# The last two token tiles of the q, k, v projection made key first, and the late key rows ahead of the values' copy

## The chip, the cores and the metric

The kernel runs on one core of a Trainium2 chip. The metric is the device time of one execution in microseconds (us), and the kernel's time is the median of several. Five engines work side by side, each with a queue of its own that it goes through in order: TensorE (PE in the profile, its weight loads PEld), VectorE (DVE), ScalarE (ACT), GpSimd (POOL) and SyncE (SP). SP, POOL and, rarely, ACT also issue the DMAs. A tile in PSUM is written by TensorE and has to be read out ("evicted") before its bank is used again.

## What is computed

A transformer block with modulation by a condition, for x of 2 x 2048 x 576 in float32, 16 heads of 36:

```python
xn = _ln(x, 1e-06)
xn = xn * (1 + sc_msa[:, None, :]) + sh_msa[:, None, :]
qkv = (xn @ w_qkv + b_qkv).reshape(B, N, 3, H, hd)
q, k, v = (qkv[:, :, 0], qkv[:, :, 1], qkv[:, :, 2])
q = _ln(q, 1e-05, qn_g, qn_b)
k = _ln(k, 1e-05, kn_g, kn_b)
attn = jnp.einsum('bqhd,bkhd->bhqk', q, k) * scale
attn = jax.nn.softmax(attn, axis=-1)
o = jnp.einsum('bhqk,bkhd->bqhd', attn, v).reshape(B, N, C)
o = o @ w_proj + b_proj
x = x + g_msa[:, None, :] * o
...
h = jax.nn.gelu(xn2 @ w1 + b1, approximate=False)
m = h @ w2 + b2
x = x + g_mlp[:, None, :] * m
```

The change lies where the making of q, k and v ends and attention begins, once in each of the two batches, and in one place near the end of batch 0's attention.

## The kernel before

**Projection** (`inputs`, lines from L1045). A batch has 2048 tokens in 16 tiles of 128 (NT = 16). For each tile TensorE makes three products, q, k and v (`product`, L1101 and L1103), each in two halves of 288 columns, into a PSUM tile `s` of two banks; there are four such tiles in turn. The weights have been centred, so that the mean of each head is already zero and the normalization needs only the variance:

- `biased` (L1115 for q and k, L1118 for v): VectorE evicts a product, adding the bias. q and k go to `both`, v goes straight to its place for attention, `vt`.
- `squared` (L1055): ScalarE squares q and k into `sq`, of which there is one buffer.
- `head_scale` (L1060 to L1067): VectorE sums the squares of each head (`var`), ScalarE takes the root, VectorE the reciprocal (`inv`), and POOL multiplies q and k by it.
- `by_feature` (L1080, L1082): VectorE transposes blocks of 32 x 32 into `turned_qk` (three buffers), and four DMAs write the rows by feature to a DRAM tensor, `qk`. They are issued by SP, or by POOL where the call says so.

Of tile t, `head_scale` runs one tile later and `by_feature` two tiles later. Key rows are read back from DRAM block by block (`take_k_block`: tiles 0-3, 4-7, 8-11, 12-13, 14-15) by SP's DMAs (L812, L814), to `km0` (32 of the 36 features of each head) and `ke0` (the other four). The DMAs are issued behind the writes of the block's last tile (for tiles 12-13 behind those of tile 14), and `take_k_block` returns a function, `made`, that applies gain and bias (L847) and splits `ke` in a high and a low part (L847, L856, L857): four VectorE operations. A list, `taken`, keeps such functions. A later `by_feature` with `ready=True` runs what is in it; with `ready=False` it doesn't. For the last tile the order is k, q, v, and its key rows are written apart from its q rows, by POOL's queue. The functions for tiles 12-13 and 14-15 are left over and returned to attention.

**Attention** (`attend`, L1228 to L1291) goes through 8 pairs of heads (p), 4 blocks of 512 queries (qb) and 4 groups of keys (g): 128 steps. Step (p, qb, g) computes the scores of two blocks of 128 keys from each half of the sequence: tiles 2g, 2g + 1, 8 + 2g and 9 + 2g. So the first two steps want tiles 8 to 11, the third 12 and 13, the fourth 14 and 15. Scores go to banks of PSUM taken from a ring of eight (`bank`), four per block of keys; ScalarE takes the exponentials to `pt` (L1232, five buffers of two); the products with `vt` (L1241) come one step behind the scores, into the next bank of the ring, and VectorE adds them to `ot` (L1291, or a copy, L1289, for the first group). VectorE's other work in attention is kept in a list, `later`, that says at the end of which step it is put in the queue; `hooks` holds further work by step. The two left functions came in through the hook of step (0, 0, 0) and went to the front of `later` for the next two turns: each behind the copy or add of the step. The closing 1/sum of a query block is `divided` (L1260, L1261).

**Order.** In both stages the order on VectorE and POOL is that of the source (a manual schedule), in the projection also on SP, in attention also on ScalarE. The rest is ordered by the scheduler. Buffers and banks are handed out as the scheduler sees them come free. Near the end of batch 0's attention three tiles of the next batch's input get their statistics (L1327, L1328) at steps (7, 2, 0), (7, 2, 1) and (7, 2, 2); `rows_turned` uses them after the last step.

Of the kernel before, what the change touches and what calls it, by code (L numbers as in the profile page):

```python
# [8 lines left out]
F32 = mybir.dt.float32  # L9
# [7 lines left out]
P = 128  # L17
# [14 lines left out]
def dit_block(  # L32
# [25 lines left out]
    nc = tc.nc  # L58
    B, N, C = x.shape
# [3 lines left out]
    NT = N // P  # L63
# [688 lines left out]
    def block_of_small():  # L752
# [292 lines left out]
        def inputs(b, weights, making, work, xnts, turned, loaded):  # L1045

            wq, wq4, bq = weights
            both, squares, taken = {}, {}, []
            key_blocks = {3: (0, 4), 7: (4, 8), 11: (8, 12), NT - 2: (12, 14), NT - 1: (14, NT)}

            def squared(t, w0=0, w1=2):
                if squares.get("t") != t:
                    squares.update(t=t, sq=work.tile([P, 2 * C], F32, name="sq", bufs=1))
                part = slice(w0 * C, w1 * C)
                nc.scalar.activation(squares["sq"][:, part], both[t][:, part], AF.Square)  # L1055

# [108 lines left out]
                    q = two_steps(0, t) if t == 0 else product(0, t)  # L1165
                    biased(0, q, t)

            for t in range(NT - 1):
                modulated_ahead(t)
                begun(t)  # L1170
                if t >= done:
                    q = product(0, t)
                k = product(1, t) if t >= done else two_steps(1, t)
                if t >= done:
                    biased(0, q, t)
                if b == 0 and t == 0:
                    xnts[done] = input_loaded(turned.pop(done), nc.gpsimd)
                    turned_ahead(t + 1)
                turned_ahead(t)
                biased(1, k, t)  # L1180
                if t > 0:
                    head_scale(t - 1)
                if t >= done:
                    v = product(2, t)
                    biased(2, v, t)
                if b == 0 and t == TPB + 1:
                    kept()
                if t >= 2:
                    by_feature(t - 2)
                squared(t)  # L1190

            t = NT - 1
            k, q, v = (product(w, t) for w in (1, 0, 2))
            head_scale(t - 1)
            by_feature(t - 2)
            biased(1, k, t)
            squared(t, 1, 2)
            head_scale(t, 1, 2)
            by_feature(t - 1, ready=False)
            biased(0, q, t)  # L1200
            squared(t, 0, 1)
            by_feature(t, 1, 2, ready=False, queue=nc.gpsimd)
            head_scale(t, 0, 1)
            biased(2, v, t)
            by_feature(t, 0, 1, ready=False)
            return taken

        NG = NT // 4

        def attend(b, pool, hooks):  # L1210

            def scores(p, qb, g):
                i, j = p % 2, qb % 2
                pts = []
                for k0 in (2 * g * P, (2 * g + 1) * P):
                    keys = slice(k0, k0 + P)  # L1220
                    banks = [bank() for _ in range(4)]
                    for k, q, first in (
                        (km[i], qm[j], True),
                        (ke[i].bitcast(F32R), qe[j].bitcast(F32R), False),
                    ):
                        for r0, ps in zip(range(0, P, 32), banks):
                            r = slice(r0, r0 + (DIMS if first else 4 * (HD - DIMS)))
                            nc.tensor.matmul(ps, k[r, keys], q[r, :], start=first, stop=not first)  # L1228
                    for c in range(2):
                        pt = pool.tile([P, 2, BLK], F32, name="pt", bufs=5)  # L1230
                        for h in range(2):
                            nc.scalar.activation(pt[:, h, :], banks[2 * c + h], AF.Exp, scale=SCALE)  # L1232
                        pts.append((pt, k0 // P + c * NT // 2))
                return pts

            def values(p, pts):
                acc = bank()
                for pt, kc in pts:
                    for h in range(2):
                        v0 = (kc * H + 2 * p + h) * HV  # L1240
                        nc.tensor.matmul(  # L1241
                            acc[64 * h : 64 * h + 64, :],
                            vt[:, v0 : v0 + 64],
                            pt[:, h, :],
                            start=pt is pts[0][0],
                            stop=pt is pts[-1][0],
                        )
                return acc

            def finish(p, qb, ot):  # L1250


                den = pool.tile([P, BLK], F32, name="den")
                for h in range(2):
                    sums = den_dram[b, p, qb, h, :]
                    nc.sync.dma_start(out=sums.unsqueeze(0), in_=ot[64 * h + HD : 64 * h + HD + 1, :])
                    nc.sync.dma_start(out=den[64 * h : 64 * h + 64, :], in_=sums.partition_broadcast(64))

                def divided():
                    nc.vector.reciprocal(den, den)  # L1260
                    nc.vector.tensor_tensor(ot, ot, den, ALU.mult)  # L1261
                    cols = slice(qb * BLK, (qb + 1) * BLK)
                    for h in range(2):
                        for c, row, d, n in head_rows((2 * p + h) * HD):
                            for r in (row,) if c < FULL else (row, row + 64):
                                nc.sync.dma_start(
                                    out=held["qo"][r : r + n, c, cols], in_=ot[64 * h + d : 64 * h + d + n, :]
                                )

                return divided  # L1270

            steps = [(p, qb, g) for p in range(NPAIR) for qb in range(NBLK) for g in range(NG)]


            behind, later = None, [[] for _ in range(13)]
            for p, qb, g in [*steps, (None, None, None)]:
                pts = None if p is None else scores(p, qb, g)
                if g == 0 and (p, qb) != (NPAIR - 1, NBLK - 1):
                    for i, do in enumerate(take_q(*((p, qb + 1) if qb + 1 < NBLK else (p + 1, 0)))):
                        later[1 + i].append(do)  # L1280
                if g == 1 and qb == 0 and p + 1 < NPAIR:
                    for i, do in enumerate(take_k(p + 1)):
                        later[3 + NG * i].append(do)
                if behind is not None:
                    bp, bqb, bg, bpts = behind
                    acc = values(bp, bpts)
                    if bg == 0:
                        ot = pool.tile([P, BLK], F32, name="ot", bufs=2)
                        nc.vector.tensor_copy(ot, acc)  # L1289
                    else:  # L1290
                        nc.vector.tensor_tensor(ot, acc, ot, ALU.add)  # L1291
                    if bg == NG - 1:
                        later[2 if bp == NPAIR - 1 else 3].append(finish(bp, bqb, ot))
                if (p, qb, g) in hooks:
                    due = hooks[p, qb, g]() or []
                    later[1] = due[:1] + later[1]
                    later[2] = due[1:] + later[2]
                later.append([])
                for do in later.pop(0):
                    do()  # L1300
                behind = (p, qb, g, pts)
            for do in [do for group in later for do in group]:
                do()
# [127 lines left out]
        for b in range(B):  # L1431
# [32 lines left out]
            def output_opened():  # L1464
                opening["wp"] = output_weights(b)

            hooks = {
                (0, 0, 0): lambda: left,
                (4, 0, 1): output_opened,
            }  # L1470
            hooks |= {
# [2 lines left out]
            if b + 1 < B:  # L1474
                begun = [(spare[5 + t], x[b + 1, t * P : (t + 1) * P, :], spare[8 + t]) for t in range(3)]

                def rows_opened():
                    opening["begun"] = rows_begun(begun)
                    for i in range(len(begun)):
                        opening["begun"][0](i)  # L1480

                def rows_turned():
                    opening["turned"] = opening["begun"][2]()

                hooks |= {(7, 1, 1): rows_opened, (None, None, None): rows_turned}
                hooks |= {
                    (7, 2 + i // NG, i % NG): lambda i=i: opening["begun"][1](i) for i in range(len(begun))
                }
            if b == 0:
                hooks |= {  # L1490
# [5 lines left out]
            with tc.manual_schedule(  # L1496
                engines={mybir.EngineType.DVE, mybir.EngineType.Pool, mybir.EngineType.Activation}
            ):
                attend(b, att, hooks)
            close_att()  # L1500
            close_psum()
            close_psum = opened_psum(s=4)
# [400 lines left out]
```

## Time and profile before

| | us |
|---|---|
| runs of the kernel | 3148.82 median of 3 (3148.65 to 3154.48) |
| the profiled execution | 3152.0 |
| its span in the profile | 3150.2 |
| TensorE's granted clock over the span | 0.999 |
| projection of batch 0, to the first score | 0 to 240.4 |
| first five steps of attention, batch 0 | 240.4 to 269.6 |
| first score of batch 1 | 1303.47 |
| DMA, mean over the span | 99 GB/s |

The costliest groups of instructions, with the sum and the mean of one, are the exponentials (L1232: 1057.6, 610 ns), the value products (L1241: 935.0, 598 ns), the scores (L1228: 571.9 and 422.1) and the projection's products (L1101: 404.9). A line of a timeline has the start, the time taken, the engine, the line of the source and the operation, output<-input, the shape, and the number of instructions merged; in brackets stands how long the engine had been idle before it, and who ended that. Matmuls are pipelined, so groups overlap a little. In a line of the busy table the three figures are busy time, share of the span and number of instructions.

### The profile page before, as it was taken

The page shows a single profiled execution, that of the slowest core. Times are in us where ns is not written, and L with a number is a line of the kernel's source. Part 1 is how long each engine was busy: PE and PEld are TensorE (multiplying, and loading weights), DVE is VectorE, ACT ScalarE, POOL GpSimd, SP SyncE. Part 2 cuts the span into 40 slices and gives each one's busy share as a digit, 9 for nine tenths or more (in the row PEclk, how much of TensorE's full clock was granted, in tenths as well). Part 3 has the DMA queues.
Part 4 walks back from the last instruction along what each step waited for, and adds up shares of the span by engine and source line. Part 5 has one row for each costly group of instructions (what it writes and reads, how often), then busy time and mean ns, then how long its engine had stood idle before and what let it go on. Part 6 is the DMA issues. An engine that isn't in the chain of part 4 may idle for free. (4 is left out here: it accounts for less than half of the span.)

```text
span 3150.2 us, 46743 instructions
## 1 busy us (share of the span) xinstructions
PE 3125.2 (99%) x17553; PEld 1862.0 (59%) x17553; DVE 1515.6 (48%) x2181; ACT 1471.2 (47%) x2843; POOL 664.2 (21%) x932
## 2 busy tenths in 40 slices
PE   8999999999999999999999999999999999999999
PEld 5883333333333788633333333368888888777777
DVE  6653443444344556434443444445566554545454
ACT  2326666666666122466666666633555541000000
POOL 4641000011110455200011111013333320112111
PEclk9999999999999999999999999999999999999999
DMA  5753221132221756411122222146554434333331
GB/s 142 179 96 95 78 64 46 54 80 73 65 74 41 244 101 123 88 45 34 44 62 68 81 65 66 56 159 188 166 132 137 136 109 165 106 121 117 117 105 39
DMA packets 300451, 311.94 MB, mean 99 GB/s; under 512 B 178936, under 2 KB 233080, under 8 KB 298104
## 3 DMA queue, kind: packets, MB, share of 16 engines
q1 hardware_dynamic: 252240, 192.19, 21.2%
q0 software_dynamic: 44432, 111.07, 13.3%
q10 hardware_dynamic: 3544, 5.60, 0.5%
q8 instruction: 141, 2.31, 0.3%
q14 instruction: 94, 0.77, 0.1%
HBM read 191.80 MB, written 106.45 MB: 95 GB/s over the span
## 5 line engine op out<-in xcount | busy, mean ns | idle before, releaser
L1232 ACT ACTIVATE pt<-b 128x512 f32<-128x512 f32 x2048 | 1057.6, 610 | 484.2 <-PE b L1241 271.2
L1241 PE MATMUL b<-pt,vt 128*64 128x512 f32 x4096 | 935.0, 598 | 0.0
L1241 PEld LDWEIGHTS b<-pt,vt 128*64 128x64 f32 x4096 | 271.8, 136 | 582.1 <-issue 438.8
L1228 PE MATMUL b<-qm,km 32*128 32x512 f32 x4096 | 571.9, 614 | 1.0 <-issue 1.0
L1291 DVE TENSOR_TENSOR ot<-b,ot 128x512 f32<-128x512 f32 x192 | 132.8, 692 | 617.5 <-PE b L1241 617.5
L1228 PE MATMUL b<-qe,ke 16*128 16x512 f32 x2048 | 422.1, 788 | 0.0
L1101 PE MATMUL s<-wq,xnt 128*128 128x288 f32 x1536 | 404.9, 407 | 2.1 <-ACT xnt L395 2.1
L1228 PEld LDWEIGHTS b<-qm,km 32*128 32x128 f32 x4096 | 192.3, 184 | 276.8 <-ACT pt L1232 215.6
L1815 PE MATMUL s<-ws,as 128*128 128x288 f32 x1440 | 351.8, 406 | 0.0
L1101 PEld LDWEIGHTS s<-wq,xnt 128*128 128x128 f32 x1536 | 281.5, 190 | 64.7 <-ACT xnt L395 1.6
L1815 PEld LDWEIGHTS s<-ws,as 128*128 128x128 f32 x1440 | 273.6, 190 | 75.6
L1260 DVE RECIPROCAL den<-den 128x512 f32<-128x512 f32 x64 | 213.6, 3337 | 11.1 <-DMA den<-den_dram 11.1
L1655 PE MATMUL m<-xnt,wb 128*128 128x256 f32 x864 | 210.4, 379 | 1.6 <-issue 0.9
L1655 PE MATMUL m<-s,wb 128*128 128x256 f32 x864 | 210.0, 379 | 0.0
L1005 POOL DMA_DIRECT2D turned<-squares x212 | 142.5, 678 | 259.0 <-DVE squares L1000 241.0
L1655 PEld LDWEIGHTS m<-s,wb 128*128 128x128 f32 x864 | 164.2, 190 | 22.3
L1228 PEld LDWEIGHTS b<-qe,ke 16*128 16x128 f32 x2048 | 107.8, 184 | 115.9 <-issue 112.0
L1289 DVE COPY ot<-b 128x512 f32<-128x512 f32 x64 | 44.3, 692 | 272.7 <-PE b L1241 272.7
L1655 PEld LDWEIGHTS m<-xnt,wb 128*128 128x128 f32 x864 | 158.9, 190 | 21.3 <-issue 1.3
L1693 ACT ACTIVATE cs<-cs,b_sb 128x512 f32<-128x512 f32 x144 | 98.9, 719 | 111.8 <-DVE cs L1688 85.8
L812 POOL DMA_DIRECT2D km<-qk x56 | 28.2, 503 | 571.7 <-PE b L1228 568.8
L1022 ACT ACTIVATE xnt<-xnt,mod 128x128 f32<-128x128 f32 x244 | 100.4, 481 | 102.1 <-DMA xnt<-turned 94.6
(206 smaller groups left out, 2941.0 us busy)
## 6 DMA issues: line engine op xcount, KB each, us to landing
gelu<-cs SPq DMA_DIRECT2D x144, 256.0 KB
hidden<-gelu SPq DMA_DIRECT2D x16, 2304.0 KB
x_dram<-spare POOLq DMA_DIRECT2D x64, 288.0 KB, 2.5
qk<-turned_qk SPq DMA_DIRECT2D x120, 144.0 KB
qm<-qk SPq DMA_DIRECT2D x256, 64.0 KB
den<-den_dram SPq DMA_DIRECT2D x128, 128.0 KB
turned<-squares POOLq DMA_DIRECT2D x212, 72.0 KB, 2.5
xnt<-turned POOLq DMA_DIRECT2D x54, 256.0 KB, 4.1
```

What stands on the lines that cost most here:

```text
L1005: queue.dma_start(out=by_square[g], in_=squares[g * SQ : (g + 1) * SQ, :].rearrange("p (k j) -> p k j", j=SQ))
L1022: nc.scalar.activation(part, part, AF.Identity, **affine(which, k, b))
L1101: nc.tensor.matmul(out_a, full[:, k, :], wq[:, k, f], start=k == 0, stop=False)
L1228: nc.tensor.matmul(ps, k[r, keys], q[r, :], start=first, stop=not first)
L1232: nc.scalar.activation(pt[:, h, :], banks[2 * c + h], AF.Exp, scale=SCALE)
L1241: nc.tensor.matmul(acc[64 * h : 64 * h + 64, :], vt[:, v0 : v0 + 64], pt[:, h, :], start=pt is pts[0][0], stop=pt is pts[-1][0],)
L1260: nc.vector.reciprocal(den, den)
L1289: nc.vector.tensor_copy(ot, acc)
L1291: nc.vector.tensor_tensor(ot, acc, ot, ALU.add)
L1655: nc.tensor.matmul(out_m[m], wb[:, slot[m], k, f * P : (f + 1) * P], moving[m](k), start=k == 0 and m in (1, 2, 5, 6), stop=k == 1 and m == 1,
L1693: nc.scalar.activation(part, part, AF.Gelu, bias=b1_sb[:, g : g + 1])
L1815: nc.tensor.matmul(ms[m], stationary[m][:, f, :], ws[m][:, f, :], start=(f == 0), stop=(f == HF - 1))
```

## The change

For tiles 14 and 15 together, the products are made in the order k, k, q, q, v, v. Tiles 13, 14 and 15 are written to DRAM in two parts, keys and q, with the keys first; tile 15's keys still go by POOL's queue. The rows of tiles 8 to 11 are made by VectorE between tile 15's key transpose and tile 14's q statistics. v is evicted last: tile 14's after tile 14's q transpose, tile 15's after tile 15's. `squared` takes a new tile for each part. In attention, the two functions that are left over are put in VectorE's queue right after the scores of steps (0, 0, 0) and (0, 0, 1). In the program that is built, both stand ahead of the copy of step 0's values. The third tile's statistics move from step (7, 2, 2) to (7, 2, 3). SP's queue, which nothing orders by hand in attention, has batch 0's first gate weights (`wa`) and their biases ahead of the loads of the third q block, where one part of `wa` and the biases stood behind them. The compiled order of buffers has tile 14's q transposed into the buffer that tile 15's key rows are written from.

```diff
             def squared(t, w0=0, w1=2):
-                if squares.get("t") != t:
-                    squares.update(t=t, sq=work.tile([P, 2 * C], F32, name="sq", bufs=1))
+                if squares.get("t") != (t, w0):
+                    squares.update(t=(t, w0), sq=work.tile([P, 2 * C], F32, name="sq", bufs=1))
...
-            for t in range(NT - 1):
+            for t in range(NT - 2):
...
-            t = NT - 1
-            k, q, v = (product(w, t) for w in (1, 0, 2))
-            head_scale(t - 1)
-            by_feature(t - 2)
-            biased(1, k, t)
-            squared(t, 1, 2)
-            head_scale(t, 1, 2)
-            by_feature(t - 1, ready=False)
-            biased(0, q, t)
-            squared(t, 0, 1)
-            by_feature(t, 1, 2, ready=False, queue=nc.gpsimd)
-            head_scale(t, 0, 1)
-            biased(2, v, t)
-            by_feature(t, 0, 1, ready=False)
+            t0, t1 = NT - 2, NT - 1
+            modulated_ahead(t0)
+            k0, k1, q0, q1 = (product(w, t) for w in (1, 0) for t in (t0, t1))
+            head_scale(t0 - 1)
+            by_feature(t0 - 2, ready=False)
+            biased(1, k0, t0)
+            squared(t0, 1, 2)
+            by_feature(t0 - 1, 1, 2, ready=False)
+            head_scale(t0, 1, 2)
+            biased(1, k1, t1)
+            squared(t1, 1, 2)
+            by_feature(t0, 1, 2, ready=False)
+            head_scale(t1, 1, 2)
+            biased(0, q0, t0)
+            squared(t0, 0, 1)
+            by_feature(t1, 1, 2, ready=False, queue=nc.gpsimd)
+            v0 = product(2, t0)
+            key_rows = [*taken]
+            for do in key_rows[:-2]:
+                do()
+            head_scale(t0, 0, 1)
+            biased(0, q1, t1)
+            squared(t1, 0, 1)
+            by_feature(t0 - 1, 0, 1, ready=False)
+            v1 = product(2, t1)
+            head_scale(t1, 0, 1)
+            by_feature(t0, 0, 1, ready=False)
+            biased(2, v0, t0)
+            by_feature(t1, 0, 1, ready=False)
+            biased(2, v1, t1)
+            taken = key_rows[-2:]
             return taken
...
-        def attend(b, pool, hooks):
+        def attend(b, pool, hooks, key_rows):
...
                 pts = None if p is None else scores(p, qb, g)
+                if (p, qb) == (0, 0) and g < len(key_rows):
+                    key_rows[g]()
...
             hooks = {
-                (0, 0, 0): lambda: left,
                 (4, 0, 1): output_opened,
             }
...
                 hooks |= {
-                    (7, 2 + i // NG, i % NG): lambda i=i: opening["begun"][1](i) for i in range(len(begun))
+                    (7, 2, (0, 1, 3)[i]): lambda i=i: opening["begun"][1](i) for i in range(len(begun))
                 }
...
-                attend(b, att, hooks)
+                attend(b, att, hooks, left)
```

## The prediction

> **What bounds the kernel now.** I read the busy table first, then the start times of TensorE's groups around each place the change touches, then what ended the waits there. Times are us of the profiled execution, for batch 0; batch 1 repeats them 1063.07 later.
>
> ```profile
> PE 3125.2 (99%) x17553; PEld 1862.0 (59%) x17553; DVE 1515.6 (48%) x2181; ACT 1471.2 (47%) x2843; POOL 664.2 (21%) x932
> ```
>
> TensorE bounds the whole, so only time in which it is held up counts. Its 99% hides such time, since a matmul that has begun counts as busy while the next one's weights wait. So I read the pitch of attention's steps, from one group of value products (L1241) to the next, in TensorE's timeline:
>
> ```profile
> 248.28 3.65 PE L1241 MATMUL b<-pt,vt 128*64 128x512 f32 x16
> ...
> 255.98 3.65 PE L1241 MATMUL b<-pt,vt 128*64 128x512 f32 x16
> ...
> 263.67 3.65 PE L1241 MATMUL b<-pt,vt 128*64 128x512 f32 x16
> ...
> 269.64 3.65 PE L1241 MATMUL b<-pt,vt 128*64 128x512 f32 x16
> ...
> 275.64 3.65 PE L1241 MATMUL b<-pt,vt 128*64 128x512 f32 x16
> ```
>
> Two pitches are 7.70 and 7.69, the next 5.97 and 6.00. The timelines of the weight loads and of VectorE tell why:
>
> ```profile
> 254.45 0.18 PEld L1228 LDWEIGHTS b<-qe,ke 16*128 16x128 f32 x2 [0.81 <-DVE ke L857]
> ```
> ```profile
> 252.01 0.69 DVE L1289 COPY ot<-b 128x512 f32<-128x512 f32 x1 [3.24 <-PE b L1241]
> 252.74 0.42 DVE L847 TENSOR_SCALAR km<-km,gb_at 64x256 f32<-64x256 f32 x1
> ...
> 253.91 0.48 DVE L857 SCALAR_TENSOR_TENSOR ke<-ended,part,high 64x256 fp32r<-64x256 f32 x1
> ```
>
> Step 2's scores need the keys of tiles 12 and 13. VectorE makes them in four operations that stand behind the copy of step 0's values, and that copy waits for TensorE. So TensorE waits for work that is queued behind a wait for TensorE. Step 3 (tiles 14, 15) repeats it.
>
> Before that, ScalarE starts late, as its timeline shows; the exponentials pace the first two steps:
>
> ```profile
> 241.30 0.31 ACT L1063 ACTIVATE var<-var,eps 128x16 f32<-128x16 f32 x1 [0.82 <-DVE var L1060]
> 241.63 1.28 ACT L1232 ACT_TABLE_LOAD   x1
> 242.92 5.01 ACT L1232 ACTIVATE pt<-b 128x512 f32<-128x512 f32 x10
> ```
>
> **The change, part by part.**
>
> *Key rows ahead of the copy.* Nothing is removed; two groups of four VectorE operations go ahead of L1289. Gain: 7.70 + 7.69 - 2 x 5.98 = 3.43 in batch 0; batch 1's pitches, 7.67 and 7.66, give 3.37. **6.80** in all, if the rows are made before step 2's scores (some 250.8 in the new time).
>
> *The order k, k, q, q, v, v.* TensorE does the same six products of 4.41 from 214.01 to 240.47. It needs tile 15's input at 218.42 instead of 227.24; POOL's last operation on it ends at 215.9. The last q leaves TensorE at 231.65 instead of 236.06, so the normalization ends earlier. I followed the compiled order on each queue with the rows' durations (evict 0.72, half a tile's transpose 0.75, its reduce 0.75, from reduce to reciprocal's end 1.4, POOL's product 1.16):
> - SP is free of tile 11's writes and the loads behind them at 224.04. Tile 12's four writes then take 2.9, as tile 11's did (216.12 to 219.02); the load that waited for those began 2.9 later (221.91). Landed: 229.9.
> - Tile 15's keys, normalized by 227.2, wait for the buffer of tile 12's transposed rows, so they are transposed 229.9 to 230.65 and written from POOL's queue. That write now takes 7.5 from the end of its transpose (240.44) to the release shown below, 6.8 in batch 1. Landed: 237.5 to 238.2.
> - Meanwhile VectorE makes keys 8 to 11 (2.33), reduces tile 14's q, evicts tile 15's (234.3) and ends with the last reciprocal at 237.2. ScalarE's last root is at 236.6.
>
> The table load then runs under the products of v, and the first exponential waits only for its scores: 1.46 after their start, as in a later step (267.25 to 268.71), at 240.40 + 1.46 = 241.86 instead of 242.92. **1.06** in batch 0; batch 1 the same (1305.99 against 1303.47 + 1.46). The Trainium skill (ScalarE: Activation LUTs, "What ACT_TABLE_LOAD costs") prices such a switch at 1.28 plus a drain of 1.38, 2.66 in all. Here the load is 1.28, and from root to exponential there is 1.31 with no drain. By the page up to 2.4 would be late; by the row 1.06 is, and I take the row.
>
> *The added wait.* Now VectorE's transpose of tile 15's q waits for POOL's write, with the copy of v ahead of it:
>
> ```profile
> 241.81 0.69 DVE L1118 TENSOR_TENSOR vt<-s,bq 128x576 f32<-128x576 f32 x1
> 247.99 0.78 DVE L1080 STREAM_TRANSPOSE turned_qk<-both 128x576 f32<-128x576 f32 x1 [5.48 <-DMA qk<-turned_qk]
> ```
>
> In the new order it is the transpose of tile 14's q that takes that buffer and waits, and *both* copies of v are queued behind it. The first score takes the PSUM bank of tile 14's v; TensorE waits for that copy. Transpose at 238.2, copy 238.9 to 239.6 (or 0.7 earlier, by batch 1's write): 0.8 to 1.5 ahead of 240.40. Tile 15's copy follows at 240.5 to 241.2, and its bank is wanted by the second block of keys at 241.4. I cost this wait at 0. If the cover is gone, each us beyond it costs a us per batch. The trace doesn't show this write beside its new neighbours: at best nothing is late; at worst I let it land 2 later than now, which costs up to 1.2 per batch.
>
> *More, smaller writes.* Per batch, SP's and POOL's row writes go from 20 to 28, 24 of them of 72 KB. The Trainium skill (DMA: Bandwidth & Descriptors, "Anatomy of one DMA" and "Rules for kernel authors") speaks against that: about 2 us fixed for each DMA, so coalesce. Read as queue time, eight more cost 16, and the late keys would come after step 3 wants them. The rows show that issue goes on while earlier writes land: four of 72 KB take 2.7 on SP (250.15 to 252.87; 2.2 in batch 1), four of 144 KB take 2.9. So SP gets one group of 2.9 and five of 2.5, 15.4, where it had three of about 3.0 and one of 2.5, 11.5: 4 more. They lie thus: tile 13's and 14's keys 227.0 to 232; loads of keys 12, 13 to 235 or 236; loads of keys 14, 15 wait for POOL's landing, 238.2 to 240.4 (2.1, as at 247.92 to 250.04), and land by 243 to 244. VectorE makes both groups (1.65 each) by 246.3 at the latest, over 4 ahead of need. Three groups of q rows follow to 248, then the loads of the next q block, landed by 252.5; VectorE's next add is due at 256.8, so they cost 0. POOL's loads of the next pair's keys start some 4.6 earlier and stay off the path. The weights for the gates now go ahead of the loads of the third q block; 2.36 MB at the 400 GB/s of that stretch (windows 260 to 263) is 6, those loads end by about 268, and VectorE wants them at 275. Cost 0.
>
> *The third tile's statistics one step later (L1327, end of batch 0 only).* VectorE's and TensorE's timelines there:
>
> ```profile
> 986.53 0.81 DVE L1327 BATCH_NORM_STATS2 st<-spare 128x6 f32<-128x288 f32 x2
> ...
> 989.33 3.34 DVE L1260 RECIPROCAL den<-den 128x512 f32<-128x512 f32 x1
> ...
> 993.32 0.68 DVE L1291 TENSOR_TENSOR ot<-b,ot 128x512 f32<-128x512 f32 x1
> ```
> ```profile
> 988.19 3.65 PE L1241 MATMUL b<-pt,vt 128*64 128x512 f32 x16
> ...
> 995.34 3.65 PE L1241 MATMUL b<-pt,vt 128*64 128x512 f32 x16
> ```
>
> Pitch 7.15: the add that frees the bank is late by the statistics' 1.02 on top of the reciprocal. The same step of the block before, without them, has 6.10 (964.16 to 970.26). Gain **1.05**; a step later VectorE idles 5.04 before its add and hides them.
>
> *Sum:* 6.80 + 2 x 1.06 + 1.05 = **9.97** off 3152.0 (span 3150.2, and 1.8 around it), 3142.0 for an execution like the profiled one. That one lies 3.2 above the median of the runs shown, so the forecast is 3148.82 - 9.97 = **3138.9**. Everything after the places is TensorE's chain, so it moves up whole.
>
> **Rivals.**
> - *The copies of v are late, in part.* For it: POOL's release waits are 5.48 and 4.73 now, and 0.8 is a thin cover. Against it: the write starts 9.8 earlier. With the landing 3.5 later than I have it, attention starts 2 to 2.7 late in each batch: 3148.8 - 10 + 5 = 3144.
> - *The same wait decides, and the kernel is slower.* One mechanism, on VectorE between the last reciprocal and tile 14's v copy. The gain at the start of attention is 4.46 per batch, and 1.05 besides; with a cover of 1.15 it is lost when the write lands 6.1 late (13.5 from transpose to landing where now it takes 6.8 to 7.5). At 10 late: 3148.8 - 10 + 2 x 8.85 = 3156.5. No row shows such a landing.
> - *The stall only changes its releaser:* TensorE would wait for ScalarE's exponentials in steps 2 and 3. Then the load and the statistics alone remain, 3148.8 - 3.2 = 3145.6. Against it: eight exponentials take 4.0 (ten in 5.01) of a 5.98 step, and the step after the stalls is already at 5.97.
>
> **How the numbers follow.** What a measurement here can tell from no change is 0.2%, 6.3. Forecast 0.78; late in part 0.11 (half of it beyond 6.3 gained); changed releaser 0.05; slower 0.06. That gives faster 0.83, same 0.11, slower 0.06. The range reaches up to the late case, 3144. Downwards little is left to gain: the first score can't come before 240.40, so only the roughness of the terms (pitches read to 0.1, six of them, and the 1.46) and the scatter of executions remain, together taken as 1.9: 3137.
>
> **What would show it.** Right: pitches from step 0's values on all near 6.0, their first group at 247.2; the table load ended before 240; no wait of TensorE on L1118; the pitch at step (7, 2, 2) 6.1. Wrong: a gap ahead of the first score with VectorE's v copy as releaser, or a 7.7 pitch with a DMA of key rows behind it.

## The result, and the profile after

The changed kernel takes 3138.78 us (median of 6 runs, 3138.53 to 3139.57) against 3148.76 for the kernel before (6 runs on the same chip): 9.98 less, a ratio of 0.9967 with a 95% interval of 0.9957 to 0.9977. The forecast was 3138.9. The profiled execution of the changed kernel took 3139.02, with a span of 3137.1 and a granted clock of 0.999.

TensorE's timeline of the changed kernel, the value products (now L1258) of the first five steps in batch 0:

```profile
244.20 3.65 PE L1258 MATMUL b<-pt,vt 128*64 128x512 f32 x16
250.18 3.65 PE L1258 MATMUL b<-pt,vt 128*64 128x512 f32 x16
256.16 3.65 PE L1258 MATMUL b<-pt,vt 128*64 128x512 f32 x16
262.13 3.65 PE L1258 MATMUL b<-pt,vt 128*64 128x512 f32 x16
268.13 3.65 PE L1258 MATMUL b<-pt,vt 128*64 128x512 f32 x16
```

All pitches are now 5.97 to 6.00; the two of 7.7 are gone. VectorE's timeline around the copy of step 0's values (now L1308):

```profile
238.34 0.47 DVE L847 TENSOR_SCALAR km<-km,gb_at 64x256 f32<-64x256 f32 x1
...
241.20 0.48 DVE L857 SCALAR_TENSOR_TENSOR ke<-ended,part,high 64x256 fp32r<-64x256 f32 x1
247.93 0.69 DVE L1308 COPY ot<-b 128x512 f32<-128x512 f32 x1 [6.25 <-PE b L1258]
```

The rows of tiles 14 and 15 are ready at 241.7, before the copy even begins to wait; VectorE then idles 6.25, and nobody waits for what is behind it. ScalarE's timeline at the start of attention:

```profile
234.67 0.31 ACT L1063 ACTIVATE var<-var,eps 128x16 f32<-128x16 f32 x1 [0.82 <-DVE var L1060]
235.00 1.28 ACT L1249 ACT_TABLE_LOAD   x1
238.83 5.00 ACT L1249 ACTIVATE pt<-b 128x512 f32<-128x512 f32 x10 [2.55 <-PE b L1245]
```

The table load is over at 236.28, ahead of the first score at 237.44, and the exponentials wait for TensorE (2.55) where they followed the load at once. And TensorE's timeline at step (7, 2, 2), where 7.15 has become 6.10:

```profile
980.70 3.65 PE L1258 MATMUL b<-pt,vt 128*64 128x512 f32 x16
986.80 3.65 PE L1258 MATMUL b<-pt,vt 128*64 128x512 f32 x16
```

Laid side by side by stage, from the starts of TensorE's groups in both traces (us):

| stretch | before | after | gain |
|---|---|---|---|
| first score to first values, batch 0 / 1 | 7.88 / 7.88 | 6.76 / 6.76 | 1.12 / 1.12 |
| the next three pitches together, batch 0 / 1 | 21.36 / 21.31 | 17.93 / 17.94 | 3.43 / 3.37 |
| pitch at step (7, 2, 2) | 7.15 | 6.10 | 1.05 |
| sum | | | 10.09 |

The two spans differ by 13.1, not 10.1. The other 3.0 lies before the change's reach: the projection's first product starts at 22.06 in the profiled execution before and at 19.11 in the one after. That execution of before was the one 3.2 above its median.

### The profile page after: what moved, and what is told of

Its sections match the earlier page's. It is cut to its first block, busy times and chain, and to the rows that moved or that the text cites. A ratio compares the mean times of both kernels' runs of the same rounds, so it can differ in the third digit from the quotient of the medians.

```text
span 3137.1 us, 46798 instructions
## 1 busy us (share of the span) xinstructions
PE 3113.8 (99%) x17553; PEld 1859.8 (59%) x17553; DVE 1517.1 (48%) x2189; ACT 1472.4 (47%) x2847; POOL 664.8 (21%) x934
## 4 chain that ended last, share of the span: by engine, by line
PE 98%; DVE 0%; issue 0%; DMA 0%; ACT 0%; POOL 0%; POOLq 0%; ACTq 0%
PE b L1258 29%; PE b L1245 20%; PE s L1833 16%; PE s L1101 12%; PE m L1673 12%; PE s L406 4%; PE m L1687 2%; PE one L1673 2%; PE s L1103 2%; PE s L417 0%; DMA xt<-x_dram 0%; PE b L192 0%; ACT xnt L395 0%; POOL x_dram L1400 0%; DVE wb L1602 0%
## 5 line engine op out<-in xcount | busy, mean ns | idle before, releaser
L1258 PE MATMUL b<-pt,vt 128*64 128x512 f32 x4096 | 935.0, 598 | 0.0
L1258 PEld LDWEIGHTS b<-pt,vt 128*64 128x64 f32 x4096 | 271.8, 136 | 582.1 <-issue 438.2
L1245 PE MATMUL b<-qm,km 32*128 32x512 f32 x4096 | 562.6, 613 | 0.0
L1308 DVE COPY ot<-b 128x512 f32<-128x512 f32 x64 | 44.3, 691 | 278.2 <-PE b L1258 272.9
```

What stands on the lines that cost most here:

```text
L1258: nc.tensor.matmul(acc[64 * h : 64 * h + 64, :], vt[:, v0 : v0 + 64], pt[:, h, :], start=pt is pts[0][0], stop=pt is pts[-1][0],)
```

## The experiments

Each was compared with the kernel before on the same chip. The first four of the table ran on one chip, the next four on another, and the last, with three runs that are told below it, on a third. The kernel before had a median of 3149.37, 3149.38 and 3149.52 there, 0.6 to 0.8 above the 3148.76 of the result, and the changed kernel itself, run again on the third chip, 3139.40, 0.6 above its 3138.78; so differences of 0.7 between chips mean nothing.

| run | median (range, runs) | ratio to before | first score to first values, batch 0 / 1 | next two pitches, batch 0 / 1 |
|---|---|---|---|---|
| rows behind | 3146.21 (3144.95 to 3147.43, 11) | 0.9991 [0.9981, 1.0] | 6.76 / 6.76 | 7.69, 7.70 / 7.66, 7.66 |
| rows ahead, old order | 3145.45 (3144.79 to 3148.1, 11) | 0.9988 [0.9979, 0.9997] | 7.88 / 7.88 | 7.94, 5.98 / 6.97, 5.98 |
| statistics back | 3140.33 (3139.74 to 3140.87, 7) | 0.9971 [0.996, 0.9982] | 6.76 / 6.76 | 5.98, 5.98 / 5.98, 5.98 |
| v copies first | 3138.89 (3138.49 to 3139.82, 6) | 0.9967 [0.9955, 0.9979] | 6.76 / 6.76 | 5.98, 5.98 / 5.98, 5.98 |
| keys by SP | 3140.98 (3140.63 to 3141.44, 9) | 0.9974 [0.9964, 0.9984] | 6.76 / 7.20 | 5.98, 5.98 / 5.98, 5.98 |
| keys by SP, v first | 3140.11 (3139.69 to 3140.73, 7) | 0.9972 [0.996, 0.9983] | 6.76 / 6.76 | 5.98, 5.98 / 5.98, 5.98 |
| two buffers | 3156.02 (3154.05 to 3156.74, 11) | 1.0019 [1.001, 1.0028] | 10.37 / 13.86 | 5.98, 5.98 / 5.98, 5.98 |
| four buffers | 3137.62 (3136.49 to 3139.27, 5) | 0.9965 [0.9952, 0.9979] | 6.76 / 6.76 | 5.98, 5.98 / 5.98, 5.98 |
| v ahead of the last q | 3139.19 (3138.37 to 3140.26, 6) | 0.9966 [0.9954, 0.9979] | 6.76 / 6.76 | 5.98, 5.98 / 5.98, 5.98 |

### The place in the queue alone

The order of the products stays; the key rows go back behind the copy.

```diff
-                if (p, qb) == (0, 0) and g < len(key_rows):
-                    key_rows[g]()
...
+                (0, 0, 0): lambda: left,
```

> The changed kernel, with its order k, k, q, q, v, v, but the eight operations on the late key rows put back behind the copy of step 0's values (and behind the next add). Theory (the place in VectorE's queue is worth 6.80, whatever the order): the pitches of the first two steps go back from 5.98 to 7.7 in each batch, the time from the first score to the first values stays at 6.76, and the kernel takes 3138.8 + 6.8 = 3145.6. Rival (the gain comes from the key rows landing some 10 earlier): pitches stay near 6.0 and the time at 3138.8.

VectorE's and the weight loads' timelines of this run:

```profile
248.49 0.69 DVE L1306 COPY ot<-b 128x512 f32<-128x512 f32 x1 [9.62 <-PE b L1258]
249.22 0.42 DVE L847 TENSOR_SCALAR km<-km,gb_at 64x256 f32<-64x256 f32 x1
...
250.39 0.48 DVE L857 SCALAR_TENSOR_TENSOR ke<-ended,part,high 64x256 fp32r<-64x256 f32 x1
```
```profile
250.93 0.18 PEld L1245 LDWEIGHTS b<-qe,ke 16*128 16x128 f32 x2 [0.81 <-DVE ke L857]
```

The pitches are back to 7.69 and 7.66, though VectorE sat idle for 9.62 ahead of the copy, time in which the same four operations run in the changed kernel. Against the changed kernel's trace the four pitches are 1.71, 1.72, 1.68 and 1.68 longer: 6.79, where 6.8 was expected. The median lies 7.3 above that of the run with v copied first on the same chip. The theory holds: with the data as early as in the changed kernel, the 6.8 is gone when the place is. Early data alone bring nothing to these pitches.

### The place in the queue with the old order

The projection is that of the kernel before, and so are the statistics; only `key_rows` stands ahead of the copy.

```diff
-            k0, k1, q0, q1 = (product(w, t) for w in (1, 0) for t in (t0, t1))
...
+            t = NT - 1
+            k, q, v = (product(w, t) for w in (1, 0, 2))
...
                 if (p, qb) == (0, 0) and g < len(key_rows):
                     key_rows[g]()
```

> The old order of the products (tile 15 as k, q, v, rows of q and k written together) with the eight operations ahead of the copy of step 0's values, and the old place of the third tile's statistics. Theory (the order is needed for the place to pay): the loads of the rows of tiles 14 and 15 are issued at 247.9 to 250.0 in the kernel before and land at about 252.5, so the rows are made by 254.2 and the copy behind them ends at 254.9, where it ended at 252.7; the first pitch stays near 7.7 and only the second falls to 6.0. First score to first values 7.88, statistics' pitch 7.15, time 3148.8 - 2 x 1.7 = 3145.4 (3144 to 3147). Rival (the place alone is worth 6.80): both pitches 6.0 and 3142.0.

SyncE's and VectorE's timelines of this run:

```profile
226.66 13.73 SPq L1082 DMA_DIRECT2D qk<-turned_qk  x12
240.56 2.40 SPq L812 DMA_DIRECT2D km<-qk  x1
```
```profile
249.75 0.42 DVE L847 TENSOR_SCALAR km<-km,gb_at 64x256 f32<-64x256 f32 x1 [3.60 <-DMA km<-qk]
...
252.72 0.48 DVE L857 SCALAR_TENSOR_TENSOR ke<-ended,part,high 64x256 fp32r<-64x256 f32 x1
253.24 0.69 DVE L1291 COPY ot<-b 128x512 f32<-128x512 f32 x1
```

VectorE now waits 3.60 for the loads, and the copy, queued behind, is late itself: the first pitch is 7.94, the second 5.98. In batch 1 the loads came earlier against the step, and the first pitch is 6.97; the expected 7.7 was met in neither batch, and the median meets the expected 3145.4 in part because the two misses have opposite signs. So of the 6.80 the place alone brings 3.9 against the kernel before (3149.37 to 3145.45), and the rest needs the keys written early. The table load also ends here, as before, behind the first score (at 240.21, with the score at 237.71): 7.88.

### The statistics

```diff
-                    (7, 2, (0, 1, 3)[i]): lambda i=i: opening["begun"][1](i) for i in range(len(begun))
+                    (7, 2, i): lambda i=i: opening["begun"][1](i) for i in range(len(begun))
```

> The changed kernel with the third tile's statistics back at the end of step (7, 2, 2). Theory: the pitch there goes from 6.10 to 7.15 and the time to 3138.8 + 1.05 = 3139.8. Rival (the statistics only move the wait to the start of batch 1): the pitch changes, but batch 1 starts as much earlier, and the time stays at 3138.8.

TensorE's timeline of this run, for the pitch that was 6.10:

```profile
980.79 3.65 PE L1258 MATMUL b<-pt,vt 128*64 128x512 f32 x16
987.92 3.65 PE L1258 MATMUL b<-pt,vt 128*64 128x512 f32 x16
```

7.13, 1.03 more than the changed kernel's, and from there to its end the trace stays that much later; the medians are 1.4 apart on one chip (3140.33 against 3138.89 of the next run). The stall doesn't come back elsewhere.

### The added wait

```diff
+            biased(2, v0, t0)
             by_feature(t0, 0, 1, ready=False)
-            biased(2, v0, t0)
+            biased(2, v1, t1)
             by_feature(t1, 0, 1, ready=False)
-            biased(2, v1, t1)
```

> The changed kernel with both copies of v ahead of the transpose that waits for a buffer (tile 14's copy ahead of tile 14's q transpose, tile 15's ahead of tile 15's). Theory (the added wait is covered, costed at 0): the copy of tile 14's v ends earlier than now, the first score comes at the same time, 3138.8 +- 0.5. Rival (the wait already costs some of the start): the first score comes up to 0.5 earlier per batch, 3137.8.

The two copies of the changed kernel (first fence, VectorE's timeline) and of this run (second):

```profile
235.22 0.78 DVE L1080 STREAM_TRANSPOSE turned_qk<-both 128x576 f32<-128x576 f32 x1
235.92 0.72 DVE L1118 TENSOR_TENSOR vt<-s,bq 128x576 f32<-128x576 f32 x1
```
```profile
235.07 0.69 DVE L1118 TENSOR_TENSOR vt<-s,bq 128x576 f32<-128x576 f32 x1
235.69 0.76 DVE L1080 STREAM_TRANSPOSE turned_qk<-both 128x576 f32<-128x576 f32 x1
```

In the changed kernel the transpose has no idle time in brackets: the rows written from its buffer had left (SP issues the loads that wait for them at 234.69). So VectorE doesn't wait there at all. The copy ends at 236.64, 0.80 ahead of the first score. Here it ends at 235.76, and nothing is gained. The added wait costs 0, and the copy has a cover of 0.8.

The next two runs were meant to take that cover away for tile 15's copy by writing tile 15's keys from SyncE's queue, without and with the copies moved ahead.

```diff
-            by_feature(t1, 1, 2, ready=False, queue=nc.gpsimd)
+            by_feature(t1, 1, 2, ready=False)
```

> The changed kernel with tile 15's key rows written by SP's queue instead of POOL's. They stand there behind the loads of the rows of tiles 12 and 13, which are issued until 232.8, so they go out from about 232.9 to 235.2 and land at about 238.5, where POOL's landed by 235.2. Tile 14's q now takes another buffer; the transpose of tile 15's q takes the one that these rows leave from, and the copy of tile 15's v is queued behind it. Theory (each us that a copy of v is late beyond the need of its bank costs a us per batch): transposed 238.5 to 239.3, copied by 240.0, where the second block of keys wants that bank 1.0 after the first score, at 238.45: 1.5 late in each batch, 3138.8 + 3.0 = 3141.8 (3140 to 3145). Rival (a covered wait): 3138.8.

> As the run with tile 15's keys by SP's queue, but with both copies of v ahead of the transposes. The late landing stays, but no copy of v is queued behind a wait for it. Theory: the time comes back to 3138.8 +- 0.6, since the rows of tiles 14 and 15 are still made by about 246, ahead of their step. Rival (the late landing itself costs, through the key rows): as long as the run without the copies moved.

VectorE's and the weight loads' timelines in batch 1 of the run without the copies moved, whose first score is at 1295.11:

```profile
1294.50 0.42 DVE L847 TENSOR_SCALAR km<-km,gb_at 64x256 f32<-64x256 f32 x1
...
1296.19 0.78 DVE L1080 STREAM_TRANSPOSE turned_qk<-both 128x576 f32<-128x576 f32 x1
1296.89 0.72 DVE L1118 TENSOR_TENSOR vt<-s,bq 128x576 f32<-128x576 f32 x1
```
```profile
1297.66 0.20 PEld L1245 LDWEIGHTS b<-qm,km 32*128 32x128 f32 x3 [1.16 <-DVE vt L1118]
```

Tile 15's copy is late, but not through the wait that was expected. The transpose ahead of it has no idle time: in batch 0 the rows had left by 236.49, when SP issues their loads, and not at 238.5. In this build VectorE's queue has the four operations on the rows of tiles 12 and 13 (1294.50 to 1296.16) ahead of that transpose, and they make the copy late. So the run shows the price of a late copy, not that of a late write. The second block of keys stands 1.16 for the copy, yet the first values come only 0.44 late; in batch 0, where that copy ended at 239.53 behind a first score at 237.64, they come in time. ScalarE still has exponentials of the first block to do, so the second block has some 0.7 more cover than I gave it. With the copies moved ahead both starts are as in the changed kernel. But the medians of both runs lie higher than that explains (the second's above its 3138.8 +- 0.6, and the first's is in its range for another reason than the one given): behind the first product of the output projection the trace of the first is 1.6 longer than the changed kernel's, of the second 1.9, at the start of the MLP, which the edit doesn't touch. Part of this is scatter, as the changed kernel's second trace shows below.

```diff
-                turned_qk = work.tile([P, 2 * C], F32, name="turned_qk", bufs=3)
+                turned_qk = work.tile([P, 2 * C], F32, name="turned_qk", bufs=2)
```

> The changed kernel with two buffers for the transposed rows instead of three. Each half tile waits for the writes of the half tile two before it; tile 14's q waits for POOL's write of tile 15's keys, which itself starts some 2 later, and in VectorE's queue three operations on the key rows of tiles 12 and 13 stand ahead of it; the copy of tile 15's v comes behind the operations on the rows of tiles 14 and 15, which wait for their loads. Theory (the price of a late copy of v is 1 us per us and batch): tile 14's copy ends at about 240.5, 3 late; tile 15's not before 244, some 5 to 6 late in all; 3138.8 + 2 x 5.5 = 3150 (3145 to 3154), above the kernel before. The first score and the second block of keys start within 0.1 of the ends of the copies. Rival (the pipeline takes up part of a late start, since ScalarE and VectorE run below their limits): under 3144.

VectorE's and the weight loads' timelines of this run, and its windows of the start of attention (PE, PEld, DVE, ACT and POOL busy, then the granted clock, the DMA share and GB/s):

```profile
227.89 0.78 DVE L1080 STREAM_TRANSPOSE turned_qk<-both 128x576 f32<-128x576 f32 x1 [5.81 <-DMA qk<-turned_qk]
```
```profile
242.23 0.70 PEld L1245 LDWEIGHTS b<-qm,km 32*128 32x128 f32 x8 [4.63 <-DVE vt L1118]
...
246.93 0.30 PEld L1245 LDWEIGHTS b<-qm,km 32*128 32x128 f32 x3 [2.07 <-DVE vt L1118]
```
```profile
241.00:242.00 1.00, 0.00 (x0) 0.00 (x0) 1.00 (x2) 0.00 (x0) 1.00 (x3) 0.61 0.83 169
242.00:243.00 1.00, 0.77 (x4) 0.70 (x8) 0.97 (x4) 0.00 (x0) 1.00 (x3) 0.50 1.00 185
...
250.00:251.00 1.00, 1.00 (x11) 0.49 (x7) 0.00 (x0) 1.00 (x3) 0.40 (x2) 0.50 0.51 131
251.00:252.00 1.00, 1.00 (x17) 0.76 (x10) 0.00 (x0) 0.93 (x3) 0.00 (x0) 0.77 0.36 93
252.00:253.00 1.00, 1.00 (x11) 0.24 (x7) 0.00 (x0) 0.30 (x1) 0.00 (x0) 1.00 0.80 217
```

Both copies of v are late in batch 0, and the weight loads wait 4.63 and 2.07 for them in a row. With this the kernel is slower than before: late copies of v can cost more than the change gains, as the rival that was to end slower had it, but its path isn't the one seen. No late write of POOL's holds tile 14's q transpose, which has no idle time ahead of it. VectorE had already stood 5.81 for a buffer ahead of tile 14's key transpose (the first fence), its last reciprocal ended at 238.91 where the changed kernel's ended at 235.26, and operations on key rows stand ahead of the transpose as well. The median lies outside the expected 3145 to 3154. Counted from the end of the projection, the first values come 8.1 (batch 0) and 7.1 (batch 1) late, where 5 to 6 was expected. Part of the difference is probably the clock: with TensorE idle for 4.39 it fell to half speed and stayed there for some 10, and the first exponential came 2.54 after its first score (244.77 and 242.23) where it comes 1.39 after it in the changed kernel. How much of the 8.1 is the clock's wasn't separated. The two starts make 15.2 of the 16.8 between the spans of the two traces; another 1.3 lies at the start of the MLP, as in the two runs above.

```diff
-                turned_qk = work.tile([P, 2 * C], F32, name="turned_qk", bufs=3)
+                turned_qk = work.tile([P, 2 * C], F32, name="turned_qk", bufs=4)
```

> The changed kernel with four buffers for the transposed rows instead of three; VectorE's order is the same. The transpose of tile 15's keys needs no wait for tile 12's writes, so they go out and land earlier, but it is now tile 13's q that takes the buffer they are written from, five operations ahead of tile 14's q, and the reciprocal of the last q stands behind that transpose. Theory: POOL's write is issued from about 226 and lands at about 232.5, as tile 13's q comes up in the queue at 232 to 233, so nothing is late and the time is 3138.8 +- 0.6. Rival (POOL's write starts no earlier): transposed at 235.2 to 236.0, last reciprocal at 237.7, copy of tile 14's v at 239.1, first score 1.7 late, 3138.8 + 3.4 = 3142.2.

Nothing is late at either start, as the theory had it. The wait is now at the transpose of tile 13's q (2.79), where it is covered. The median was 1.2 below the changed kernel's on another chip, and below the expected 3138.8 +- 0.6, so three kernels were run beside each other:

> The changed kernel once more, beside the next two on the same chip, as their measure. Theory: 3138.8 +- 0.6; the tail behind batch 1's last values 1074.1 as before.

> The run with four buffers once more. Its first run was 1.2 below the changed kernel, 0.9 of it in its trace at the end of batch 1's attention, where the first product of the output projection did not wait for the last add. Theory (the banks were handed out differently, so this is the program's): 0.9 to 1.2 below the changed kernel on this chip again. Rival (scatter of the opening and of that place): equal within 0.5.

> The run with keys by SP's queue and v copied first once more. Its first run was 1.3 above the changed kernel though both starts of attention were the same in its trace; the 1.8 arose at the start of the MLP. Theory (it is that program's, from the order of later transfers): 1.3 above the changed kernel on this chip again. Rival (the chip, or scatter): equal within 0.5.

The changed kernel took 3139.40 (3137.33 to 3140.08, 6 runs), four buffers 3139.26 (3138.27 to 3142.52, 6), keys by SP with v first 3140.68 (3140.46 to 3141.32, 7). The last is 1.3 above the changed kernel for the second time, and each of its runs is longer than each of the changed kernel's. Its trace has only 0.3 more behind the first product of the output projection than the changed kernel's (1074.35 against 1074.05), and the two traces differ by 0.6 in all, since the changed kernel's profiled execution was its longest here (3140.08). So where the 1.3 lies stays open. The same stretch of the changed kernel was 1073.20 in its first trace: 0.9 of scatter in one program, so of the 1.6, 1.9 and 1.3 above no more than a part can be put down to the edits. Four buffers can't be told from three: in both of its traces the weight loads of the output projection's first product are spared the wait of 1.7 for the last add of attention, and that product starts 0.9 sooner behind the last values, yet the gain didn't show in the median a second time.

### What brings the first exponential forward

The prediction put this down to the last q's earlier place among the products. This run gives the place back and keeps the rest (with the copies of v first):

```diff
-            k0, k1, q0, q1 = (product(w, t) for w in (1, 0) for t in (t0, t1))
+            k0, k1, q0 = product(1, t0), product(1, t1), product(0, t0)
+            v0 = product(2, t0)
+            q1 = product(0, t1)
```

> As the run with both copies of v first, but with the products in the order k, k, q, v, q, v: the last q leaves TensorE one product (4.41) later, at the old distance from the end of the projection, while the keys keep their early place. Theory (the 1.1 at the start of attention comes from the last q alone, through root and table load): the first exponential again comes some 2.5 after the first score, first score to first values goes from 6.76 to 7.9, the pitches stay at 6.0, and the time is 3138.9 + 2 x 1.1 = 3141.1. Rival (it comes from the early keys, or from the evictions of v): 6.76 and 3138.9.

Its VectorE timeline, against the same eviction in the kernel before (second fence):

```profile
233.02 0.76 DVE L1115 TENSOR_TENSOR both<-s,bq 128x576 f32<-128x576 f32 x1 [0.59 <-PE s L1103]
```
```profile
237.80 1.32 DVE L1080 STREAM_TRANSPOSE turned_qk<-both 128x1152 f32<-128x1152 f32 x1
239.04 0.72 DVE L1115 TENSOR_TENSOR both<-s,bq 128x576 f32<-128x576 f32 x1
```

The theory falls: 6.76 and 3139.19, as if the q were early. It left TensorE 4.4 later, and VectorE took it as it came, waiting 0.59 for it. Even in the changed kernel the early q isn't used early. Its TensorE line (the second half of that product) and VectorE's eviction of it:

```profile
228.05 0.65 PE L1103 MATMUL s<-wq,xnt 128*128 128x288 f32 x2
```
```profile
232.38 0.69 DVE L1115 TENSOR_TENSOR both<-s,bq 128x576 f32<-128x576 f32 x1
```

It is out at 228.70 and waits 3.7 for VectorE, which is busy but for 0.37. In the kernel before the q was out at 236.06 and evicted only at 239.04, with no idle time ahead of the eviction: it stood in VectorE's queue behind the transposes. VectorE had idled 2.37, 3.65 and 1.65 between 214 and 228 there, and was busy from then on but for short waits for ScalarE and the squares. In the changed kernel, transposes, reduces and reciprocals of the keys run in the time in which it idled. By these traces, what brought the table load forward is the work moved earlier in VectorE's queue. Which of the moves suffices wasn't tried.

## Why the prediction was right, and where not

- **Key rows ahead of the copy, 6.80:** 3.43 + 3.37 in the traces, and 6.79 when the place alone is undone. Right, as was the condition that the rows are made in time: 241.7, where my latest (246.3) becomes 243.3 when 2.96 is taken off for the earlier opening.
- **The start of attention, 1.06 per batch:** 1.12 and 1.12. The size and the row it was read from hold: 1.28 for the table load and no drain, since in the kernel before the exponential followed 0.01 after it; the first exponential now comes 1.39 after its score, where 1.46 was taken. The step that failed is its reason: "The last q leaves TensorE at 231.65 instead of 236.06, so the normalization ends earlier." The run with v ahead of the last q shows that it may leave at the old time. VectorE's backlog was the limit, and I had looked at the product's end without asking when it was evicted (239.04, three later); the last root and reciprocal came 1.0 to 1.3 later than worked out, which the table load's cover took up.
- **The added wait, 0:** the cost is right, and so is POOL's landing: 237.5 to 238.2, less 2.96, where the rows had left by 234.69. But there was no wait: VectorE reached tile 14's q transpose only at 235.22, a us later than worked out, and that set the copy's place. That the cover of 0.80 is the low end of my 0.8 to 1.5 is chance. The price "each us beyond it costs a us per batch" is too simple: tile 15's copy, 1.16 late for its bank, cost 0.44, and the long stall with two buffers, where the clock fell, cost more than expected.
- **More, smaller writes, 0:** right; tile 12's writes started at 221.14, as worked out (224.04 less 2.96), and landed 0.8 later than I had them; tile 15's key transpose waited 2.64 for them, and TensorE waited for nothing behind it. The loads of the next q block had landed by 250.67, a us later than worked out and still 3.2 ahead of the add behind them. The 2 us that the prediction cites against small writes from the Trainium skill (DMA: Bandwidth & Descriptors, "Anatomy of one DMA") are given there for DMAs that GpSimd issues, and put down mostly to completion. The eight more are SP's, so the page doesn't price them, and to read its figure as queue time was too much.
- **The gate weights ahead of the third q block's loads, 0:** those loads were issued until 264.6, and VectorE's operation on them, at 272.47, has no idle time ahead of it but the one for TensorE's products.
- **Statistics, 1.05:** 1.05, and 1.03 when undone.
- **The rivals:** the copies of v weren't late, and no stall changed its releaser. That late copies can make the kernel slower than before took two buffers to show, and there they were late by an earlier wait, not by POOL's write.

Sum: 9.97 predicted, 10.09 between the traces, 9.98 between the medians, and 10.12 between those of the third chip (3149.52 and 3139.40). That 9.97 and 9.98 agree to 0.01 is chance; the terms are good to some 0.1. To set the profiled execution's own 3.2 aside was right: 3.0 of it is in the opening.

## What to carry to other kernels

Where an engine's queue has work for the bound engine behind a wait for the bound engine, the work goes ahead of the wait, but only if its data is there first: the place alone was worth 3.9, with the earlier writes 6.8. A "99% busy" engine can hide such stalls, and the pitch between equal groups of work shows them. When a result is late, look at when it was evicted, not only at when it was produced.

## What was not expected of the hardware

A stall of TensorE can have a price beyond its length. In the run with two buffers TensorE was idle from 237.84 to 242.23 in batch 0, and from 1304.60 to 1307.87 in batch 1. Its timeline, and its windows in batch 1 (columns as above):

```profile
242.23 2.08 PE L1245 MATMUL b<-qm,km 32*128 32x512 f32 x6 [4.39 <-DVE vt L1118]
...
1307.87 1.22 PE L1245 MATMUL b<-qm,km 32*128 32x512 f32 x1 [3.26 <-DVE vt L1118]
...
1311.41 1.23 PE L1245 MATMUL b<-qm,km 32*128 32x512 f32 x3 [1.04 <-DVE vt L1118]
```
```profile
1306.00:1307.00 1.00, 0.00 (x0) 0.00 (x0) 0.97 (x2) 0.00 (x0) 1.00 (x3) 0.59 0.90 134
...
1316.00:1317.00 1.00, 1.00 (x14) 0.43 (x8) 0.00 (x0) 0.48 (x1) 0.00 (x0) 0.79 0.18 55
```

Read from the shares in these windows of 1 us, the granted clock fell to 0.50 at some 241.2 and came back at some 251.5; in batch 1 it fell at some 1306.2 and came back at 1316.4. Both stretches of half clock are 10.2 long, though the second stall is the shorter one, and though the profile counts TensorE as busy through most of them. The Trainium skill (TensorE: Matmul & The Clock Gate, "Part 1: The HAM clock gate") has the fall after one idle window of some 3.4 and the return after one busy window of as much. The return agrees in both batches: counted in windows of 3.4 from the fall, the first still holds the stall and the second another wait of TensorE (0.49 and 1.04), and the third, without one, ends where the clock comes back. By the page's rule it was then the second, short wait that kept the clock down for one window more; no run here shows that by itself. The fall agrees in batch 0 only, 3.4 after TensorE had gone idle; in batch 1 it came 1.6 after, and why isn't shown. Idle stretches of up to 0.90, as ahead of the MLP's first product in the changed kernel, left the clock at 1.00.
